# Squared lengths of keys and queries by four 32-column matmuls on partitions of their own

## The chip, the cores and the metric

The kernel runs on one core of one Trainium2 chip. The metric is the device time of one execution in microseconds (us); for the kernel before, it is the median of three runs. The profile that is quoted below comes from a further, profiled execution of the same kernel.

## The reference

Two graph layers work on 1250 nodes with 512 features and 20000 edges. The first one, a convolution over the edges beside an attention with random features, holds the change. Of its attention, this part matters here (`t` stands for the keys or the queries, 8 heads of 64 features, `proj` has 256 rows):

```python
def phi(t, is_query):
    t = t * scale                                   # scale = DH ** (-0.25)
    u = jnp.einsum('bhnd,md->bhnm', t, proj)
    diag = 0.5 * jnp.sum(t * t, axis=-1, keepdims=True)
    if is_query:
        m_ = jnp.max(u, axis=-1, keepdims=True)
    else:
        m_ = jnp.max(u, axis=(-2, -1), keepdims=True)
    return jnp.exp(u - diag - jax.lax.stop_gradient(m_)) / np.sqrt(M) + KEPS
qf = phi(q, True)
kf = phi(k, False) * mask[:, None, :, None]
```

Half the squared length of a head's vector, `diag`, is what the change touches. Only 256 token slots take part in the attention (all nodes have batch number 0, and a slot number is at most 255), so keys, queries and values are computed for 256 tokens. Around this stand layer norms, the sum over edges as a product with an adjacency matrix, the convolution's product, batch norms, and a second layer with two large products.

## The kernel before, in words

A first part sorts out the edges (lines above 1400). Then `sorted_graph` builds the adjacency matrix `adj` in 25 batches of 50 columns: `onehots` makes two one-hot tiles on VectorE (L206), `count` multiplies them on TensorE (ten matmuls, L217), and ScalarE casts the sums into `adj` (L220). The attention's preparation is a generator, `beside`, whose pieces stand between these batches in the text of the program:

- `first_nodes` and `node` turn the normed rows of x into `hT`, features on partitions (`transposed`: four transposes, L226, and a copy on ScalarE, L227; the layer norm's statistics are on VectorE, L96 to L101).
- `features(ed.wk, "k")`: for each block b of 128 features, four matmuls of `wk` with `hT` into a PSUM tile (L245); ScalarE scales it into `tT` (L249) and squares it into `sq` (L251). A matmul with the columns of `half` sums the squares of each of the block's two heads (L248, L253) into rows 2b and 2b+1 of `pd`; the four blocks accumulate in `pd`, 8 partitions by 256 tokens. The matmul of block b-1 stands behind the four matmuls of block b. `pd` is copied to `d8` (L255), turned by two transposes (L259) and copied into `dg` (L260).
- eight `pairs`: scores of the keys (L267, two matmuls with 64 rows each), a copy into `kf` (L333), the maximum `kmx` (L334), a matmul for the values (L337), and statistics of `hT` (`stats`, L325).
- `km1` (L347), its largest value over all tokens (L352, L354, L362) and with it `kb` (L365); `features(wqt, "q")` for the queries; between its pieces the exponentials of `kf` on ScalarE (L376, sixteen of them), and the first two `xn` tiles (`normed`, L289).

Behind that, ten turns of a loop do `query` (L267, L461 to L466), `product` (hw, L422, into a PSUM tile of the pool with two buffers that `count` uses too), `keyvalue` (L449), `degrees` (L431 to L438), `batch`, `turn` (L472) and `attend` (L482).

The order of instructions on an engine is fixed when the kernel is built. `order` (`tc.keep_in_program_order`) pins an instruction behind the one that stands before it in the program on its engine; an instruction without it is placed by the framework's scheduler, which follows the program's order but takes a later instruction when it reckons that an earlier one isn't ready. The eight matmuls with `half` are not pinned. An fp32 matmul appears in the profile as two passes, each a LDWEIGHTS and a MATMUL. The PSUM tiles of this part come from the pool `mm` with four buffers; `sq` and `d8` share one tag of two buffers in SBUF.

Of the kernel before, what the change touches and what calls it, by code (L numbers as in the profile page):

```python
# [11 lines left out]
F32 = mybir.dt.float32  # L12
# [4 lines left out]
AF = mybir.ActivationFunctionType  # L17
# [6 lines left out]
KD = D // 128  # L24
KH = HID // 128
TOK = 256
HEADS, DH, M = 8, 64, 256
# [13 lines left out]
NT = TOK // 128  # L41
# [28 lines left out]
def sorted_graph(ctx: ExitStack, tc: tile.TileContext, ed, x, n1g, n1b, n2g, n2b, wconv, bconv,  # L70
                 wq, wk, wv, wo, proj, eps, w1, b1, g1, be1, w2, b2, g2, be2, out):
    nc = tc.nc
# [5 lines left out]
    ident, epsc = ed.ident, ed.epsc  # L78
    order = tc.keep_in_program_order
# [69 lines left out]
    ap1 = att.enter_context(tc.tile_pool(name="att", bufs=1))  # L149
    ap2 = att.enter_context(tc.tile_pool(name="att2", bufs=2))  # L150
    mm = att.enter_context(tc.tile_pool(name="mm", bufs=4, space=PSUM))
# [33 lines left out]
    wct = weight(wconv, "wconv", ap1, "wconv")  # L185


    half = ap1.tile([128, KD, HEADS], F32, name="half")
    nc.gpsimd.memset(half, 0.0)
    for b in range(KD):  # L190
        for a in range(2):
            nc.gpsimd.memset(half[a * 64:a * 64 + 64, b, 2 * b + a:2 * b + a + 1], 0.5)
    va = ap1.tile([128, NT, HEADS, DH + 1], F32, name="va")
    nc.gpsimd.memset(va, 1.0)

# [40 lines left out]
    def features(wt, name):  # L236

        tT = ap1.tile([128, KD, TOK], F32, name=f"{name}T", tag="tT")
        dg = ap1.tile([128, NT, HEADS], F32, name=f"{name}_dg")

        pd = mm.tile([HEADS, TOK], F32, name="mm")
        for b in range(KD):
            ps = mm.tile([128, TOK], F32, name="mm")
            for k in range(KD):
                nc.tensor.matmul(ps, wt[:, k, b * 128:(b + 1) * 128], hT[:, k, :TOK],  # L245
                                 start=(k == 0), stop=(k == KD - 1))
            if b:
                nc.tensor.matmul(pd, half[:, b - 1, :], sq, start=(b == 1), stop=False)  # L248
            nc.scalar.activation(tT[:, b, :], ps, AF.Copy, scale=DH ** -0.25)  # L249
            sq = ap2.tile([128, TOK], F32, name="sq")  # L250
            nc.scalar.activation(sq, tT[:, b, :], AF.Square)  # L251
            yield
        nc.tensor.matmul(pd, half[:, KD - 1, :], sq, start=False, stop=True)  # L253
        d8 = ap2.tile([HEADS, TOK], F32, name="d8", tag="sq")
        nc.scalar.copy(d8, pd)  # L255
        yield
        ps = mm.tile([128, NT, HEADS], F32, name="mm")
        for t in range(NT):
            nc.tensor.transpose(ps[:, t, :], d8[:, t * 128:(t + 1) * 128], ident[:HEADS, :HEADS])  # L259
        nc.vector.tensor_copy(dg, ps)  # L260
        return tT, dg

    def scores(tT, t, b):
# [28 lines left out]
    def beside():  # L292
# [9 lines left out]
        def node():  # L302
            for j in more:
                nodes([j])
                break

        keys = features(ed.wk, "k")
        try:
            while True:
# [36 lines left out]
        km1 = ap1.tile([128, HEADS], F32, name="km1")  # L346
        nc.vector.tensor_tensor(km1, kmx[:, 0, :], kmx[:, 1, :], ALU.max)  # L347
        queries = features(wqt, "q")
        next(queries)
        stats(len(steps))  # L350
# [160 lines left out]
    for f in range(KD):  # L511
        ps = mm.tile([128, TOK], F32, name="mm")
# [5 lines left out]
    for b in range(KD):  # L518
        ps = mm.tile([128, TOK], F32, name="mm")
# [11 lines left out]
    mm = ctx.enter_context(tc.tile_pool(name="mm2", bufs=8, space=PSUM, reuse_waits="tile"))  # L531
# [33 lines left out]
    for f in range(KD):  # L565
        fs = slice(f * 128, (f + 1) * 128)
        st = tmp.tile([128, 3, 6], F32, name="st")
        for i, (n0, n) in enumerate(BSPLIT if f == KD - 1 else ESPLIT):
            c = slice(n0, n0 + n)
            ps = banks.pop(0)[:, :n] if banks else mm.tile([128, n], F32, name="mm")  # L570
            for part in (hi, lo):
                if part is lo and i == 1 and f > 0:
                    add_rows(f - 1)
                for j, k in enumerate(ROWS):
                    nc.tensor.matmul(ps, part[:k, j, fs], adj[:k, j, c],  # L575
                                     start=(part is hi and j == 0), stop=(part is lo and j == NJ - 1))
            t = p2.tile([128, n], F32, name="t", bufs=3)
            nc.vector.tensor_tensor(t, ps, rdeg[:, c], ALU.mult)

            b = at["bconv"] + f  # L580
# [43 lines left out]
    for g in groups:  # L624
        ps = mm.tile([S, 4, 128], F32, name="mm")
# [282 lines left out]
    a, b = (Dense(ops2, m, KD // 2, o, "b2") for m in range(2))  # L908
# [490 lines left out]
def tile_gnn(ctx: ExitStack, tc: tile.TileContext, x, src, dst, *rest):  # L1399
# [171 lines left out]
    with tc.If(v == 0) as arms:  # L1571
        sorted_graph(tc, ed, x, *rest)
# [33 lines left out]
```

## Time and profile before

| | before |
|---|---|
| median of 3 runs | 376.24 us (375.83 to 377.05) |
| the profiled execution | 377.66 us, of it 375.9 us from the first to the last instruction |
| instructions | 4922 |
| TensorE matmuls (PE) | 357.0 us busy, 95% of the span |
| TensorE weight loads (PEld) | 263.3 us, 70% |
| VectorE (DVE) | 235.6 us, 63% |
| ScalarE (ACT) | 157.4 us, 42% |
| GpSimd (POOL) | 35.4 us, 9% |
| granted TensorE clock | 0.989 of full speed |

A row of a profile names a line of the kernel, an engine, an operation and tiles as out<-in; "128*8 128x256" at a matmul is 128 rows and 8 columns of the array and a moving operand of 128 partitions by 256 elements. Ends of matmuls are modelled, so how long a pass takes is read from the distance between starts, or from the chain of work that ended last, where parts follow each other without overlap. "0.33 <-issue" behind a row is idle time of its engine before it in which nothing that the profile shows was waited for.

### The profile page before, as it was taken

What the parts mean: (1) busy time and instruction counts of PE and PEld (TensorE: products, weight loads), DVE (VectorE), ACT (ScalarE), POOL (GpSimd) and SP (SyncE); (2) the same over time, 40 slices, a digit from 0 to 9 for tenths busy, and PEclk for the clock granted to TensorE, in tenths of its full rate; (3) what the DMA queues carried; (4) which work ended last, traced back from release to release, by engine and by line L of the source; (5) the groups of instructions that cost most, each with busy time, mean ns of one, the idle gap of its engine ahead of it and who ended that gap; (6) DMA issues with size and microseconds to landing.
All of it is one profiled execution on the core that took longest, in us unless ns stands there. A gap on an engine that the chain in (4) does not pass through costs nothing.

```text
span 375.9 us, 4922 instructions
## 1 busy us (share of the span) xinstructions
PE 357.0 (95%) x1840; PEld 263.3 (70%) x1840; DVE 235.6 (63%) x585; ACT 157.4 (42%) x310; POOL 35.4 (9%) x55
## 2 busy tenths in 40 slices
PE   8799989999999999999999999999999999999970
PEld 4665555676566699998768888777777777777750
DVE  6899994649897235687887232182780888212783
ACT  5498549727565360111157312232652542111230
POOL 3000000000000005000000009610062000000000
PEclk9999999999999999999999999999999999999995
DMA  6943020000000471000000000240000000000045
GB/s 200 289 166 128 16 98 0 2 1 2 0 1 2 151 279 67 0 3 0 0 2 0 2 0 1 55 171 0 2 0 1 1 2 0 1 0 2 10 126 144
DMA packets 13285, 18.06 MB, mean 48 GB/s; under 512 B 1341, under 2 KB 6658, under 8 KB 13254
## 3 DMA queue, kind: packets, MB, share of 16 engines
q1 hardware_dynamic: 10622, 16.41, 13.0%
q10 hardware_dynamic: 2632, 1.27, 1.3%
q8 instruction: 16, 0.26, 0.3%
q14 instruction: 15, 0.12, 0.1%
HBM read 15.11 MB, written 2.56 MB: 47 GB/s over the span
## 4 chain that ended last, share of the span: by engine, by line
PE 83%; DVE 11%; ACT 2%; issue 1%; DMA 1%; DVEq 0%
PE mm L764 29%; PE mm L707 12%; PE mm L575 12%; PE hw L422 10%; PE mm L245 3%; PE mm L449 2%; PE mm L521 2%; PE mm L482 2%; PE sc L267 2%; PE acc L217 2%; DVE op L206 1%; DVE xs L894 1%; PE mm L226 1%; PE mm L701 1%; DVE kmx L334 1%; PE mm L472 1%
## 5 line engine op out<-in xcount | busy, mean ns | idle before, releaser
L779 ACT ACTIVATE kept<-mm,vT 128x313 f32<-128x313 f32 x36 | 18.5, 521 | 49.6 <-PE mm L764 48.5
L422 PE MATMUL hw<-wconv,xn 128*128 128x512 f32 (+1 forms) x80 | 37.1, 605 | 0.3 <-ACT adj L220 0.3
L707 PE MATMUL mm<-hi,adj 128*128 128x512 f32 (+2 forms) x100 | 32.2, 400 | 0.5 <-DVE hi L655 0.4
L707 PE MATMUL mm<-lo,adj 128*128 128x512 f32 (+2 forms) x100 | 31.7, 395 | 0.0
L129 ACT ACTIVATE r<-mv,epsc 128x1 f32<-128x1 f32 x16 | 4.7, 292 | 52.1 <-DVE mv L128 52.1
L764 PE MATMUL mm<-hid,w 128*128 128x313 f32 x96 | 25.8, 427 | 0.0
L422 PEld LDWEIGHTS hw<-wconv,xn 128*128 128x128 f32 (+1 forms) x80 | 14.1, 188 | 16.4 <-issue 14.8
L575 PE MATMUL mm<-adj,lo 128*128 128x416 f32 (+3 forms) x120 | 25.1, 355 | 0.0
L575 PE MATMUL mm<-adj,hi 128*128 128x416 f32 (+3 forms) x120 | 25.1, 355 | 0.0
L206 DVE TENSOR_TENSOR op<-iop,prow 128x1280 f16<-128x1280 f16 (+2 forms) x27 | 20.8, 769 | 6.0 <-PE acc L217 5.6
L784 DVE TENSOR_TENSOR hid<-mm,kept 128x313 f32<-128x313 f32 x24 | 10.9, 477 | 20.4 <-ACT kept L779 16.9
L764 PEld LDWEIGHTS mm<-hid,w 128*128 128x128 f32 x96 | 18.2, 190 | 6.9
L575 PEld LDWEIGHTS mm<-adj,hi 128*128 128x128 f32 x120 | 21.9, 189 | 1.1
L575 PEld LDWEIGHTS mm<-adj,lo 128*128 128x128 f32 x120 | 21.8, 189 | 1.0
L707 PEld LDWEIGHTS mm<-hi,adj 128*128 128x128 f32 (+2 forms) x100 | 18.4, 186 | 5.8 <-DVE hi L655 1.4
L698 DVE SCALAR_TENSOR_TENSOR z<-h,e,mm 128x512 f32<-128x512 f32 (+1 forms) x10 | 7.0, 745 | 23.5 <-PE mm L707 15.7
L707 PEld LDWEIGHTS mm<-lo,adj 128*128 128x128 f32 (+2 forms) x100 | 18.5, 186 | 4.6 <-DVE lo L648 0.2
L217 PEld LDWEIGHTS <-op 128*128 128x128 f16 x250 | 13.7, 97 | 9.1 <-issue 4.7
L217 PE MATMUL acc<-ok,op 128*128 128x100 f16 x250 | 16.2, 208 | 3.4 <-DVE ok L206 2.7
L784 DVE TENSOR_TENSOR o<-mm,kept 128x313 f32<-128x313 f32 x12 | 5.7, 482 | 21.5 <-ACT kept L779 20.8
L702 ACT COPY zT<-mm 128x512 f32<-128x512 f32 (+1 forms) x10 | 5.3, 583 | 29.3 <-PE mm L701 29.3
L764 PE MATMUL mm<-tz,w 128*128 128x313 f32 x64 | 17.5, 426 | 0.0
(249 smaller groups left out, 717.0 us busy)
## 6 DMA issues: line engine op xcount, KB each, us to landing
w<-in_L_gnn_W_dram SPq DMA_DIRECT2D x2, 2048.0 KB
xs<-in_x_dram SPq DMA_DIRECT2D x1, 2304.0 KB
wk<-in_L_gnn_Wk_dram SPq DMA_DIRECT2D x1, 1024.0 KB
x<-in_x_dram SPq DMA_DIRECT2D x1, 1024.0 KB
v<-in_L_gnn_Wv_dram SPq DMA_DIRECT2D x1, 1024.0 KB
wconv<-in_L_gnn_W_conv_dram SPq DMA_DIRECT2D x1, 1024.0 KB
wk<-in_L_gnn_Wq_dram SPq DMA_DIRECT2D x1, 1024.0 KB
o<-in_L_gnn_Wo_dram SPq DMA_DIRECT2D x1, 1024.0 KB
```

What stands on the lines that cost most here:

```text
L206: i = nc.vector.tensor_tensor(t[:, qs], iota.unsqueeze(1).to_broadcast(shape), keys[:, bt, qs].unsqueeze(2).to_broadcast(shape), ALU.is_equal)
L217: nc.tensor.matmul(acc[:, :, q * TG:(q + 1) * TG], op[:, q, :, i], ok[:, q, :, i].rearrange("p (j t) -> p j t", t=TG), start=(q == 0 and i ...
L245: nc.tensor.matmul(ps, wt[:, k, b * 128:(b + 1) * 128], hT[:, k, :TOK], start=(k == 0), stop=(k == KD - 1))
L267: nc.tensor.matmul(ps[:, a, :M], tT[a * 64:a * 64 + 64, b, t * 128:(t + 1) * 128], projT[a * 64:a * 64 + 64, :], start=True, stop=True)
L422: nc.tensor.matmul(ps[:n], xn[:, f, :n], wct[:, f, :], start=(f == 0), stop=(f == KD - 1))
L449: nc.tensor.matmul(ps[:, i, :], kf[:, t, hd, mb * 128:(mb + 1) * 128], va[:, t, hd, :], start=(t == 0), stop=(t == NT - 1))
L482: nc.tensor.matmul(pa[:, i, :], qfTs[n][:, i, mb, :], kv[:, mb, hd, :], start=(mb == 0), stop=(mb == 1))
L575: nc.tensor.matmul(ps, part[:k, j, fs], adj[:k, j, c], start=(part is hi and j == 0), stop=(part is lo and j == NJ - 1))
L707: nc.tensor.matmul(ps[:n], adj[:k, j, t * S:t * S + n], part[:k, j, :], start=(part is hi and j == 0), stop=(part is lo and j == NJ - 1))
L764: order(nc.tensor.matmul(banks[i], left[:, k, m * 128:(m + 1) * 128], right[:, k, i * NH:(i + 1) * NH], start=(p in (1, 2, 5) and k == 0), ...
L779: nc.scalar.activation(t[:, c, :], self.A[c], AF.Identity, bias=self.part(i, 0, c)[1], scale=1.0)
L784: order(nc.vector.tensor_tensor(self.part(i, j, c)[0], self.B[c], t[:, c, :], ALU.add))
```

## The change

The four blocks no longer accumulate in one tile of 8 partitions. `half` becomes one tile of 32 columns, of which two are filled, and all blocks use it; the squares of all four blocks stay in one tile `sq`; after the last block four matmuls, each with 32 columns, write partitions 32b to 32b+31 of a `pd` with 128 partitions, pinned behind each other with `order`. The copy `d8`, the transposes and the last copy handle 128 partitions, of which the copy to `dg` takes two columns in each 32. Six of nine memsets on GpSimd go.

```diff
-    half = ap1.tile([128, KD, HEADS], F32, name="half")
+    QUAD = 128 // KD
+    half = ap1.tile([128, QUAD], F32, name="half")
     nc.gpsimd.memset(half, 0.0)
-    for b in range(KD):
-        for a in range(2):
-            nc.gpsimd.memset(half[a * 64:a * 64 + 64, b, 2 * b + a:2 * b + a + 1], 0.5)
+    for a in range(2):
+        nc.gpsimd.memset(half[a * 64:a * 64 + 64, a:a + 1], 0.5)
...
-        pd = mm.tile([HEADS, TOK], F32, name="mm")
+        sq = ap2.tile([128, KD, TOK], F32, name="sq", bufs=1)
         for b in range(KD):
             ps = mm.tile([128, TOK], F32, name="mm")
             for k in range(KD):
                 nc.tensor.matmul(ps, wt[:, k, b * 128:(b + 1) * 128], hT[:, k, :TOK],
                                  start=(k == 0), stop=(k == KD - 1))
-            if b:
-                nc.tensor.matmul(pd, half[:, b - 1, :], sq, start=(b == 1), stop=False)
             nc.scalar.activation(tT[:, b, :], ps, AF.Copy, scale=DH ** -0.25)
-            sq = ap2.tile([128, TOK], F32, name="sq")
-            nc.scalar.activation(sq, tT[:, b, :], AF.Square)
+            nc.scalar.activation(sq[:, b, :], tT[:, b, :], AF.Square)
             yield
-        nc.tensor.matmul(pd, half[:, KD - 1, :], sq, start=False, stop=True)
-        d8 = ap2.tile([HEADS, TOK], F32, name="d8", tag="sq")
+        pd = mm.tile([128, TOK], F32, name="mm")
+        for b in range(KD):
+            order(nc.tensor.matmul(pd[b * QUAD:(b + 1) * QUAD], half, sq[:, b, :], start=True, stop=True,
+                                   skip_group_check=True))
+        d8 = ap2.tile([128, TOK], F32, name="d8", bufs=1)
         nc.scalar.copy(d8, pd)
         yield
-        ps = mm.tile([128, NT, HEADS], F32, name="mm")
+        ps = mm.tile([128, NT, KD, QUAD], F32, name="mm")
         for t in range(NT):
-            nc.tensor.transpose(ps[:, t, :], d8[:, t * 128:(t + 1) * 128], ident[:HEADS, :HEADS])
-        nc.vector.tensor_copy(dg, ps)
+            nc.tensor.transpose(ps[:, t], d8[:, t * 128:(t + 1) * 128], ident)
+        nc.vector.tensor_copy(dg.rearrange("p t (b a) -> p t b a", a=2), ps[:, :, :, :2])
         return tT, dg
```

## The prediction

> **What bounds the kernel now.** I read the page's slices and the engines of its chain first, then a table of the stages around the change, then the timeline of TensorE at each place that the change touches, then who waits for whom.
>
> ```profile
> PE   8799989999999999999999999999999999999970
> ...
> DVE  6899994649897235687887232182780888212783
> ...
> PE 83%; DVE 11%; ACT 2%; issue 1%; DMA 1%; DVEq 0%
> ```
>
> A slice is 9.4 us. TensorE carries 83% of the chain that ended last, and from 53 us on hardly anything else does until the tail. So TensorE time saved early should reach the end, unless another engine sets the pace where it is saved. In slices 2 to 6, where keys and queries are made, VectorE reads 8 or 9 too. Hence the table (columns: start:end, length, then busy PE, PEld, DVE, ACT, POOL):
>
> ```profile
> 16.00:38.00 22.00, 21.38 (x147) 14.22 (x147) 20.97 (x59) 18.70 (x44) 0.77 (x7) 1.00 0.50 169
> 38.00:53.20 15.20, 13.22 (x102) 7.51 (x100) 15.06 (x35) 8.51 (x17) 0.00 (x0) 1.00 0.19 69
> 53.20:63.15 9.95, 9.70 (x60) 5.95 (x56) 4.34 (x12) 7.26 (x17) 0.00 (x0) 1.00 0.01 2
> 63.15:69.20 6.05, 6.05 (x33) 3.35 (x33) 4.87 (x9) 6.05 (x16) 0.00 (x0) 1.00 0.00 0
> 69.20:128.00 58.80, 58.77 (x359) 37.94 (x357) 41.91 (x99) 31.54 (x73) 0.00 (x0) 1.00 0.01 4
> ```
>
> The keys' features lie in the first row, the scores of the keys in the second, the queries' features in the third. In the first, TensorE is idle 0.6 us and VectorE 1.0 of 22: two full engines. In the second VectorE is full and TensorE idle for 2.0 us. In the third TensorE is full, and ScalarE is from 55.5 us on. From 63.15 to 128 TensorE is never idle.
>
> **What TensorE pays for one matmul with `half` today.** The starts show it (the granted clock is full in all these rows):
>
> ```profile
> 21.94 0.38 PE L245 MATMUL mm<-hT,wk 128*128 128x256 f32 x1
> 22.25 0.60 PE L248 MATMUL mm<-sq,half 128*8 128x256 f32 x2
> ...
> 22.25 0.10 PEld L248 LDWEIGHTS mm<-sq,half 128*8 128x8 f32 x2 [0.33 <-issue]
> 22.77 0.31 PEld L226 LDWEIGHTS mm<-ident,hn 128*128 128x128 f32 x3 [0.43 <-ACT kT L249]
> ```
>
> A pass over 256 elements takes 0.216 us (in the chain, eight passes of L245 take 1.73). The last L245 pass starts at 21.94, so the next could at 22.15; L248 starts at 22.25. Its two passes would let L226 start at 22.68; it starts at 22.77, with its weights not loaded ahead, which costs 0.06 more. So 0.43 of work carries 0.10 on the way in and 0.15 on the way out: 0.68 us. Its square had been ready since 18.7, so that is no wait for data. The keys' other three cost the same (0.68 each), the queries' four 0.62, 0.73, 0.64 and 0.63 by the same reading (at 55.43, 58.19, 60.64, 62.10). Eight make 5.3 us.
>
> The two transposes of `d8`, on 8 rows of the array, behave alike:
>
> ```profile
> 63.15 1.13 PE L422 MATMUL hw<-wconv,xn 128*128 128x512 f32 x2 [0.25 <-ACT adj L220]
> 64.20 0.29 PE L259 MATMUL mm<-ident,d 8*128 8x8 f32 x2
> 64.42 1.12 PE L422 MATMUL hw<-wconv,xn 128*128 128x512 f32 x2
> ```
>
> The two L422 passes from 63.15 on could be followed at 64.11; L422 goes on at 64.42, its first pass 0.10 slower: 0.42 us for the queries, and 0.31 for the keys by the same reading. All in all 6.0 us.
>
> **The change part by part.** *Four matmuls at once.* No row shows four groups of columns side by side. The nearest row is L267, two matmuls on two halves of the rows:
>
> ```profile
> 33.13 0.49 PE L267 MATMUL sc<-projT,kT 64*128 64x256 f32 x2
> ...
> 33.13 0.70 PE L267 MATMUL sc<-projT,kT 64*128 64x256 f32 x4
> 33.77 0.70 PE L337 MATMUL mm<-v,hT 128*128 128x512 f32 x1
> ```
>
> The first row is cut at 33.2: two passes have started by then, 7 ns apart; all four are over in time for L337 at 33.77. Two matmuls took the time of one. If columns behave like rows, one visit costs 0.10 in, 2 x 0.216, three times 0.007, about 0.03 for loading 32 columns instead of 8 (8 columns took 87 ns, 128 took 190), and 0.15 out: 0.74 us.
>
> A rule of the Trainium skill speaks against it: "TensorE: Matmul & The Clock Gate", The mechanism, says a weight load runs beside matmuls in flight only when the row group differs, and here all four use all rows. Against its wording stands L245: in one row group, at 0.216 us a pass, no load is exposed. By the rule, eight passes of 0.216 + 0.09 and 0.25 make 2.70 us a visit. The same page (Measured speedup vs the span model) gives 2.38 times for three column groups. Between lie passes that overlap only with the neighbour's (five slots: 1.36) and passes in sequence with hidden loads (2.01). I take 0.74, by the nearest row, and keep 2.70 as the other end. Switching in and out is in all of them; "TensorEngine Tiling (Array Packing)", Key Properties, says that changing the mode drains the engine, which is the 0.10 of the rows above.
>
> *Transposes.* Now 128 rows and columns, like L226, which needs 0.11 each and, outside a switch, nothing in or out: 0.22 instead of 0.42 and 0.31, although sixteen times as many elements move.
>
> *Sum on TensorE.* A features stage goes from 3.0 us to 0.74 + 0.22 = 0.96. Saved: 2.0 for keys, 2.1 for queries, 4.1 together; with 2.70 a visit, 0.2.
>
> *The rest.* The copy `d8` covers 128 partitions (0.36 us; a copy of the same 256 elements on 128 partitions, L249, 0.38): 0.04 on ScalarE in all. The last copy keeps its 16 elements (0.17). Six memsets of 0.092 leave GpSimd at 9.3 to 10.4 us; it is then idle for 8 us, so 0, and uncovered they would be a gain. No DMA moves or is added; SP passes nothing new. `pd` holds a PSUM buffer only at the end of the stage, which frees one of four before: 0 to a gain, apart from the rival below. The pin puts the first `pd` matmul behind the last of the ten L217 before it in the program; in the keys L253 already ran right behind such a group, in the queries that batch's ten were over at 61.6, before L253 at 62.10: 0. All four now wait for the last square; behind the first one on TensorE wait `d8`, the transposes and `q_dg` (65.05), which nobody needs before the query's 65.72. If VectorE or ScalarE did not cover these, the order would cost up to the 0.5 us between the squares and L253.
>
> **What of it reaches the end.** *Keys (2.0).* VectorE is the second full engine, and it waited for TensorE only here:
>
> ```profile
> DVE op L206 <- PE acc L217: 0.4, 1, 0.4
> DVE oh L431 <- PE mm L226: 0.3, 1, 0.3
> ```
>
> That 0.7 can go. Beyond it a gain needs a new order on VectorE: it runs fill-in between 37 and 49 us that belongs later (two L431 and L601, 0.9; L289, 1.7), and has 5.2 us free for it from 56.6 on. Bounds 0.3 and 2.0; I take 0.8. The next late thing is VectorE's `kmx`.
>
> *Queries (2.1).* TensorE's next large work, L422 at 63.15, takes a PSUM buffer that ScalarE frees with the cast at 62.53 (0.25 idle before it, in the fence above). ScalarE runs from 55.53 to there without a hole but 0.12 and 0.18 us before L249, and its work stays: the cast can come 0.3 earlier. The transposes inside L422's stretch give 0.2 more. Later the exponentials end at 67.0, and work that needs them (L267 at 68.56, L449 at 69.19) has some 0.8 of slack. Bounds 0.3 and 2.1; I take 0.6.
>
> Sum: 1.4 us. The profiled execution took 377.66, 1.76 more than its span of 375.9 and 1.42 more than the median; it would become 376.3, its span 374.5, and the median 376.24 - 1.4 = 374.8.
>
> **The rivals.** *B, all of it arrives* (0.12): the scheduler, seeing a free TensorE and PSUM buffer, moves query blocks into the 2.0 us that TensorE idles before 53. For it: it did so with block 0 (L245 at 45.96). Against: it left block 1 at 53.60. Gain 2.4 to 4.1; 372.9.
>
> *C, hidden or not there* (0.18): columns don't overlap (0.2 saved), or VectorE and ScalarE eat the whole. For it: both full. Time 376.2, 0.7 either way.
>
> *D, slower* (0.18): blocks of queries (1.73 us each) moved early stand in front of scores L267 between 48 and 53 us, where `kmx`, then `kb` and all exponentials hang on them. Price: the block less TensorE's holes there (0.45, 0.62, 0.80), some 1.1 a block. It decides from the second block on: 2.3 late on the exponentials, 0.8 of slack there: 1.5 slower, 377.7. Against: TensorE recovers that work after 53.
>
> **How the numbers follow.** My own sum, A, has 0.52, with 373.8 to 375.5 as its range. Under 0.3%, 1.1 us, a measurement of this kernel can't be told from no change. Faster by more: three quarters of A, all of B, a little of C: 0.54. Slower: most of D and a little of C: 0.18. The rest is 0.28. The range leaves out the best of B and the worst of D: 372.6 to 377.4.
>
> **What would show it.** Right: the four `pd` matmuls within some 30 ns at each pass, one visit of 0.7 to 0.8 us per stage, transposes at 0.11 without an idle before them, L347 (53.21) earlier by 0.8 and L422 (63.15) by 1.4, the rows after 69 shifted and otherwise alike. Wrong: visits over 1.3 us; L347 unmoved or late; a longer idle of TensorE before L422; a query block ahead of the last scores.

## The result: slower by 0.35%, and the profile after

| | before | after |
|---|---|---|
| median of 22 runs each | 376.97 us | 378.07 us |
| ratio of the runs | | 1.0035 (95% interval 1.0019 to 1.005) |
| the profiled execution | 377.66 us, span 375.9 | 377.87 us, span 376.1 |
| TensorE matmuls busy | 357.0 us | 356.4 us |
| mean granted TensorE clock | 0.989 | 0.984 |

The kernel after is slower; the prediction was 374.8 us and its range ended at 377.4. The single runs of every kernel here, the one before too, lie in two groups about 2 us apart (in the profiled ones the first L245 starts at 13.7 to 14.0 us in the lower group and at 15.4 to 16.1 us in the upper), so where single runs are compared below, the lower group of each is meant. That group has its median at 376.13 us before (376.1 to 376.2 in each later comparison) and at 377.69 us after.

The page of the kernel after, busy tenths in slices of 9.4 us, and the chain by engine:

```profile
PE   7799978999999999999999999999999999999971
...
DVE  6998985649897325687887232182780888312783
...
PEclk9999989999999999999999999999999999999995
...
PE 81%; DVE 9%; ACT 4%; DMA 1%; issue 1%; SPq 0%; DVEq 0%
```

Slice 6 (47 to 56 us) is new in two rows: TensorE reads 7, where it read 8 before, and the granted clock has an 8 in a row that was all 9 before but for the end. The start of an execution moves by up to 2.5 us from trace to trace, so places are compared from the first L245 on. Of the kernel before:

```profile
15.53 1.97 PE L245 MATMUL mm<-hT,wk 128*128 128x256 f32 x8
...
53.49 0.27 PE L352 MATMUL mm<-ident,km 128*8 128x128 f32 x1
...
53.60 1.89 PE L245 MATMUL mm<-hT,wk 128*128 128x256 f32 x8
```

The kernel after starts its first L245 at 14.00; its other rows stand further down.

| us from the first L245 | before | after | |
|---|---|---|---|
| last L245 of the keys starts | 12.25 | 10.98 | 1.27 earlier |
| L352 (the largest key value's transpose) | 37.96 | 38.97 | 1.01 later |
| first L422 | 47.62 | 49.70 | 2.08 later |
| end of the span | 360.35 | 362.08 | 1.73 later |

So the change did its work in the first 11 us, lost 2.3 us between there and L352, and lost another 1.1 us before L422; 0.35 us came back behind it. Two things happened. TensorE of the kernel after, where the keys' features end (start, length, row):

```profile
26.26 0.63 PE L252 MATMUL mm<-sq,half 128*32 128x256 f32 x6
26.82 0.66 PE L226 MATMUL mm<-ident,hn 128*128 128x128 f32 x4
27.41 0.62 PE L252 MATMUL mm<-sq,half 128*32 128x256 f32 x2
...
28.52 0.70 PE L267 MATMUL sc<-projT,kT 64*128 64x256 f32 x2
29.15 0.44 PE L259 MATMUL mm<-ident,d 128*128 128x128 f32 x2
...
30.77 0.70 PE L267 MATMUL sc<-projT,kT 64*128 64x256 f32 x2
...
33.44 0.70 PE L267 MATMUL sc<-projT,kT 64*128 64x256 f32 x2
34.06 0.66 PE L226 MATMUL mm<-ident,hn 128*128 128x128 f32 x4
34.65 0.70 PE L267 MATMUL sc<-projT,kT 64*128 64x256 f32 x2
```

Three `pd` matmuls run in the time of one, but the fourth comes in a visit of its own (a visit is a run of such matmuls with what it costs to go over to them and back). And the framework's scheduler laid out everything behind the features anew: two pairs of key scores are split. A pair together took 0.63 us (x4); each half by itself takes the same. VectorE's waits of the kernel after, from 14 to 53 us (total, times, longest), to be held against the two rows in the prediction:

```profile
DVE op L206 <- PE acc L217: 1.5, 2, 0.8
DVE kmx L334 <- ACT kf L333: 0.6, 2, 0.3
DVE k_dg L260 <- PE mm L259: 0.2, 1, 0.2
```

VectorE is idle 2.6 us between the first L245 and L352 (before: 1.2). It has 0.4 us less work there (36.4 us busy instead of 36.8; one of 24 one-hot tiles comes later), and 1.4 less 0.4 is the 1.0 us at L352.

The second thing is the clock. The same table as in the prediction, over three stretches of 3.41 us in front of and behind L352 (columns: start:end, length, busy PE, PEld, DVE, ACT, POOL, then the granted clock), of the kernel after:

```profile
46.39:49.80 3.41, 2.55 (x31) 1.57 (x29) 3.27 (x11) 1.61 (x3) 0.00 (x0) 1.00 0.55 211
49.80:53.22 3.42, 1.75 (x20) 1.06 (x17) 3.42 (x9) 1.79 (x4) 0.00 (x0) 1.00 0.00 0
53.22:56.63 3.41, 3.41 (x10) 2.23 (x8) 2.18 (x6) 0.03 (x1) 0.00 (x0) 0.50 0.02 5
```

and of the kernel before:

```profile
47.02:50.44 3.42, 2.97 (x33) 1.98 (x31) 3.42 (x8) 1.64 (x3) 0.00 (x0) 1.00 0.68 261
50.44:53.85 3.41, 1.99 (x21) 1.15 (x18) 3.41 (x9) 1.79 (x4) 0.00 (x0) 1.00 0.00 0
53.85:57.26 3.41, 3.41 (x17) 2.39 (x16) 2.38 (x7) 1.68 (x3) 0.00 (x0) 1.00 0.02 5
```

After a stretch in which TensorE was busy 1.75 us the clock is 0.50 for one stretch; after one with 1.99 us it is not. It hits the second block of the queries, which TensorE's chain cannot spare:

```profile
52.34 0.70 PE L267 MATMUL sc<-projT,qT 64*128 64x256 f32 x4 [1.05 <-DVE kmx L334]
52.97 0.27 PE L352 MATMUL mm<-ident,km 128*8 128x128 f32 x1
53.08 3.48 PE L245 MATMUL mm<-hT,wk 128*128 128x256 f32 x8
...
63.71 1.12 PE L422 MATMUL hw<-wconv,xn 128*128 128x512 f32 x2 [1.00 <-ACT adj L220]
```

The eight passes of L245 behind L352 take 3.48 us here and 1.89 us before (row at 53.60). Of the 22 runs after, 21 have a mean clock of 0.982 to 0.984, one 0.986; in the largest later comparison 70 of 75 runs before stand at 0.986 to 0.990.

### The profile page after: what moved, and what is told of

Same layout as the page of the kernel before. It is cut to its first block, busy times and chain, and to the rows that moved or that the text cites. A ratio compares the mean times of both kernels' runs of the same rounds, so it can differ in the third digit from the quotient of the medians.

```text
span 376.1 us, 4914 instructions
## 1 busy us (share of the span) xinstructions
PE 356.4 (95%) x1840; PEld 263.6 (70%) x1840; DVE 235.9 (63%) x585; ACT 157.1 (42%) x310; POOL 34.9 (9%) x49
## 3 DMA queue, kind: packets, MB, share of 16 engines
q10 hardware_dynamic: 2632, 1.27, 1.3%
## 4 chain that ended last, share of the span: by engine, by line
PE 81%; DVE 9%; ACT 4%; DMA 1%; issue 1%; SPq 0%; DVEq 0%
PE mm L764 29%; PE mm L707 12%; PE mm L575 12%; PE hw L422 10%; PE mm L245 3%; PE sc L267 2%; PE mm L521 2%; PE mm L449 2%; PE mm L482 2%; PE acc L217 2%; DVE xs L894 1%; PE mm L701 1%; PE mm L337 1%; DMA x<-in_x_dram 1%; PE mm L226 1%; PE mm L472 1%
## 5 line engine op out<-in xcount | busy, mean ns | idle before, releaser
L422 PE MATMUL hw<-wconv,xn 128*128 128x512 f32 (+1 forms) x80 | 37.0, 604 | 1.0 <-ACT adj L220 1.0
L422 PEld LDWEIGHTS hw<-wconv,xn 128*128 128x128 f32 (+1 forms) x80 | 14.1, 187 | 17.8 <-issue 14.8
L764 PE MATMUL mm<-hid,sw 128*128 128x313 f32 x64 | 17.5, 426 | 0.0
```

The source lines that it names most:

```text
L422: nc.tensor.matmul(ps[:n], xn[:, f, :n], wct[:, f, :], start=(f == 0), stop=(f == KD - 1))
L764: order(nc.tensor.matmul(banks[i], left[:, k, m * 128:(m + 1) * 128], right[:, k, i * NH:(i + 1) * NH], start=(p in (1, 2, 5) and k == 0), ...
```

## The experiments

Two theories were tried against each other. The *clock theory*: TensorE, with less to do where VectorE sets the pace, falls below some share of busy time, is given half the clock for 3.41 us, and pays for it in the next stage. The *order theory*: the new order (split pairs, late counts) starves VectorE. A third, that columns side by side are dearer than rows, fell with the traces: the `pd` passes start 7 ns apart.

### Counts issued twice, in the kernel after

```diff
-        for q in range(BG):
+        for q in [*range(BG)] * (2 if bt in (11, 12) else 1):
...
```

> The changed kernel, with the ten count matmuls (L217) of batches 11 and 12 issued twice each (the first round is overwritten), so that TensorE has 0.46 us more to do in each of its two largest holes before 53 us (0.86 before the score pair of L267 at 49.34, and 1.05 before the one at 52.34). The order of all instructions on all engines up to the second layer stays that of the changed kernel. Theory 1 (the half clock of 3.41 us that the trace shows from 53.22 on comes from TensorE's holes before it and costs about 1.1 us): the half clock is gone, L352 to L422 shrinks from 10.7 to about 9.7 us, and the time falls by 1.0 to 1.5 us, although TensorE does 0.9 us more. Rival (the half clock is a matter of the run's phase, or is hidden behind ScalarE's queue): time within 0.3 us of the changed kernel or above it.

377.49 us median, ratio 1.0009 (0.9992 to 1.0026). The second set of ten matmuls begins the sum anew, so the result does not change; TensorE has 0.9 us more to do. Its two stretches ahead of L352:

```profile
50.25:53.67 3.42, 1.95 (x28) 1.25 (x24) 3.42 (x7) 2.27 (x5) 0.00 (x0) 1.00 0.01 5
53.67:57.08 3.41, 3.26 (x17) 2.42 (x18) 3.41 (x13) 0.73 (x3) 0.00 (x0) 1.00 0.02 5
```

With 1.95 us busy the clock stays. L352 is where it was after (+38.98), so the order theory's loss is still there, but L422 comes at +48.13 instead of +49.70, and the span ends 1.37 us earlier from the first L245. The lower group's runs split by their clock: ten at 0.988 to 0.990 have a median of 376.59 us, six at 0.982 or 0.983 of 377.8 us. Doing more work made the kernel faster. What is left against before, 0.46 us by the runs and 0.36 by the traces, belongs to the order.

### Fewer counts, in the kernel before

```diff
+        last = 0 if bt in (10, 11, 12) else 1
         for q in range(BG):
-            for i in range(2):
+            for i in range(last + 1):
...
```

> The kernel before, with the counts of the batches 10, 11 and 12 halved: only one of the two matmuls of each group is issued (5 instead of 10 of L217 a batch), so that their counts are half missing. TensorE has about 0.7 us less work (15 matmuls of 0.046 us), all of it between 47 and 53.5 us, where it waits for VectorE; the order on TensorE and on VectorE stays that of the kernel before. Clock theory: TensorE's busy time in the 3.41 us before 54 us falls from about 2.0 us to about 1.5 us, the next such stretch is then granted half the clock, and the kernel gets slower by about 1 us although it does less: ratio 1.002 to 1.004, mean granted clock 0.983 instead of 0.989 in most runs. Order theory (only the sequence of the instructions matters): nothing is late, so the ratio is 0.998 to 1.000 and the clock 0.989.

378.15 us, ratio 1.0024 (1.0003 to 1.0045). Half of the counts of three batches are left out, so `adj` is incomplete. The order of TensorE is that of before and L352 stays at +37.96, to the hundredth; the clock changes:

```profile
48.79:52.20 3.41, 1.77 (x16) 1.03 (x13) 3.41 (x9) 1.76 (x4) 0.00 (x0) 1.00 0.00 0
52.20:55.62 3.42, 3.42 (x10) 1.85 (x8) 2.04 (x4) 0.44 (x2) 0.00 (x0) 0.50 0.02 5
```

L422 is 1.64 us later than before, the end 1.60 us. Ten of the 22 runs had it (most were expected to), at a mean clock of 0.978 to 0.984: in the lower group three at 377.5 to 377.6 us, beside seven at 0.986 to 0.990 with a median of 376.15 us, as before. The price of one stretch at half clock in this place is 1.4 us by the runs and 1.6 by the traces, in a kernel without any of the change. That a half-clock stretch costs the time, and that the work of TensorE ahead of it brings or removes it, is shown both ways round.

### No squared lengths at all

```diff
-            if b:
-                nc.tensor.matmul(pd, half[:, b - 1, :], sq, start=(b == 1), stop=False)
...
-        nc.tensor.matmul(pd, half[:, KD - 1, :], sq, start=False, stop=True)
...
-        nc.scalar.copy(d8, pd)
+        nc.scalar.copy(d8, sq[:HEADS])
```

> The kernel before, leaving out all eight matmuls with half (d8 is a copy of squares instead, so the squared lengths are wrong): 5.3 us less work on TensorE, more than the change saves. If TensorE sets the pace here, as the prediction had it: 2 to 5 us faster. Theory 1: the keys' part of the saving ends in holes before 53 us, a half clock follows, and the time is within 1.5 us of the kernel before. Theory 2 (slow by the changed order): faster by 2 us or more, as no pair of L267 is split in this one.

The squared lengths are then not computed at all; `d8` is a copy of squares. 378.35 us is the median of all 22 runs; the ratio, 1.0 (0.9976 to 1.0025), is that of the 15 up to 379.4 us. All eight matmuls with `half` are gone, and nothing is won, as the clock theory had it; the order theory had expected 2 us or more. L422 comes at +46.38 in the trace, 1.2 us earlier than before, in spite of this:

```profile
45.79:49.20 3.41, 1.72 (x24) 1.26 (x24) 3.41 (x6) 1.95 (x5) 0.00 (x0) 1.00 0.00 0
49.20:52.61 3.41, 3.40 (x12) 2.22 (x10) 2.58 (x9) 0.71 (x2) 0.00 (x0) 0.50 0.02 5
52.61:56.03 3.42, 3.42 (x10) 2.39 (x9) 1.33 (x5) 1.62 (x2) 0.00 (x0) 0.50 0.00 0
```

Two stretches at half clock. The runs show the staircase: the only one at 0.989 took 373.9 us, those at 0.986 and 0.982 took 374.8 and 374.9, those at 0.980 begin at 376.5, those at 0.973 at 377.9. By that one run, all the sums could bring with the clock left alone is some 2.2 us (376.1 to 373.9).

### The columns at the old places

Against the kernel before; `half`, `pd`, the copies and the transposes are those of the kernel after.

```diff
...
-                nc.tensor.matmul(pd, half[:, b - 1, :], sq, start=(b == 1), stop=False)
+                nc.tensor.matmul(pd[(b - 1) * QUAD:b * QUAD], half, sq, start=True, stop=True, skip_group_check=True)
...
```

> The kernel before, with one part of the change alone: each block's squares are summed by a matmul of 32 columns onto partitions of their own, at the place where the kernel before does it (behind the next block's four matmuls), so no visit to the array is saved and no matmuls lie side by side; copy and transposes with 128 partitions. Theory 1 (time goes where TensorE is freed): TensorE's visits are as dear as before, the time is within 0.5 us of the kernel before and there is no half clock. Theory 2 (the new order that the scheduler finds, with score pairs of L267 split in two, makes it slow): the order around the keys' scores changes here too (one pair is split), so up to 1 us slower without any half clock.

380.69 us (six runs), ratio 1.0093 (1.0059 to 1.0127), more than either theory had allowed for, though TensorE does about as much as before. Features end as before (+12.29), L352 comes at +39.84, 1.9 us late, with VectorE idle 2.8 us on the way, and the clock is halved from 53.77 on: both theories' losses without the gain. One pair of scores is split in this order too.

### Only the place

The four squares are kept and summed behind the last block, still in 8 rows, accumulating, without columns.

```diff
-            if b:
-                nc.tensor.matmul(pd, half[:, b - 1, :], sq, start=(b == 1), stop=False)
...
+        for b in range(KD):
+            order(nc.tensor.matmul(pd, half[:, b, :], sq[:, b, :], start=(b == 0), stop=(b == KD - 1)))
...
```

> The kernel before, with only the place changed: the four squares of a stage are kept, and the four half matmuls are issued after the last block as in the kernel after, but they still add up in 8 rows (no columns of the array, transposes of 8 rows). No score pair is split in its order. If columns are what costs, this one is faster than before by the early features: L352 at +37 us, ratio 0.995 to 0.998. If the new place is what costs (features done 1.3 us early, a larger hole of TensorE before 54 us, half clock), it is slower like the kernel after: ratio 1.001 to 1.004 and clock 0.983 in most runs. Order theory: about 0.999 to 1.001, since no pair is split but nothing else is won either.

377.0 us, ratio 0.9983 (0.9964 to 1.0001). Its order has no split pair, L352 comes at +37.80, the clock stays full in the profiled run, and the span ends 0.7 us earlier than before from the first L245. The nine lower runs (0.986 or more) have a median of 375.37 us, 0.8 below before. So the new place is not what costs; it wins, without any pin. Its features end as early as those of the kernel after (+10.98), and yet no pair is split: the early end alone did not bring the split order. Which of the other differences (durations, the wider transposes) tipped the scheduler stays open.

### The pairs kept together, in the kernel after

```diff
-            nc.tensor.matmul(ps[:, a, :M], tT[a * 64:a * 64 + 64, b, t * 128:(t + 1) * 128],
-                             projT[a * 64:a * 64 + 64, :], start=True, stop=True)
+            i = nc.tensor.matmul(ps[:, a, :M], tT[a * 64:a * 64 + 64, b, t * 128:(t + 1) * 128],
+                                 projT[a * 64:a * 64 + 64, :], start=True, stop=True)
+            if not qT: order(i)
```

> The kernel after, with the two score matmuls of a pair (L267, keys) kept in program order beside each other, so that none of the eight pairs is split. Order theory: the two visits to the array that the split cost (2 times 0.63 us) go, VectorE is idle about 1.2 us between 20 and 56 us instead of 2.6 us, and L352 comes at +37.8 us from the first L245 instead of +38.97 us; the time falls by about 1 us, ratio 1.000 to 1.002, and by another 1 us if the half clock goes as well. Clock theory alone: the pairs don't matter, L352 stays at +39.0 us and the ratio is 1.003 to 1.004.

375.01 us, ratio 0.9966 (0.9949 to 0.9984): one added pin turns the loss into a gain. All the key scores now stand in program order behind the `pd` matmuls. The starts of VectorE's maxima over the scores (`kmx`, one for each pair) show what changed. Of the kernel after (second pair on):

```profile
32.12 0.69 DVE L334 TENSOR_REDUCE kmx<-sc 128x2 f32<-128x512 f32 x1 [0.26 <-ACT kf L333]
...
36.00 0.69 DVE L334 TENSOR_REDUCE kmx<-sc 128x2 f32<-128x512 f32 x1 [0.31 <-ACT kf L333]
...
39.23 0.68 DVE L334 TENSOR_REDUCE kmx<-sc 128x2 f32<-128x512 f32 x1
...
42.54 0.68 DVE L334 TENSOR_REDUCE kmx<-sc 128x2 f32<-128x512 f32 x1
```

and with the pin (line numbers are one higher there; first pair on):

```profile
30.25 0.67 DVE L335 TENSOR_REDUCE kmx<-sc 128x2 f32<-128x512 f32 x1
...
33.12 0.69 DVE L335 TENSOR_REDUCE kmx<-sc 128x2 f32<-128x512 f32 x1
...
35.86 0.68 DVE L335 TENSOR_REDUCE kmx<-sc 128x2 f32<-128x512 f32 x1
...
38.67 0.68 DVE L335 TENSOR_REDUCE kmx<-sc 128x2 f32<-128x512 f32 x1
```

A pair every 2.7 to 2.9 us, against 3.2 to 3.9 from the second to the sixth pair after. VectorE waits once in the whole stretch, 0.6 us for L259, and L352 is at +37.46, L422 at +46.61, the end 1.25 us earlier than before from the first L245. The half clock is gone as well: all 22 runs are at 0.986 or 0.987, the trace shows full clock from 5 us up to the tail, and TensorE's lowest stretch in the profile ahead of L352 has 2.34 us of 3.41.

### The same pin on the kernel before

The three lines of the edit above, in the kernel before; nothing else.

> Control: the kernel before, with the same pin as in the run with the pairs kept (score matmuls of the keys in program order). No pair was split in it, so the pin moves only the first pair, from the first block of features to behind the last. Order theory with the change's own gain: nothing to win here, ratio 0.999 to 1.001, L352 at +37.6 to +38.2 us from the first L245. Rival, the gain of 0.34% came from the pin and not from the columns: ratio 0.996 to 0.998.

377.97 us, ratio 1.0022 (1.0001 to 1.0043). The pin itself wins nothing: the ten runs of the lower group without a halved clock (0.989 or 0.990) have a median of 376.66 us, 0.5 above before. Its first pair now stands behind all features, which may be the reason. Against it the pinned kernel after stands at 374.78 us: 1.9 us for the change under one and the same pin. (The profiled run lost 1.5 us to a half clock from 15.8 to 19.2 us, in the keys' features.)

### The place alone under the pin

The edit of the run with only the place, and the pin.

> The place alone under the same pin: the four half matmuls at the end of the stage without columns (8 rows, accumulating), and the pairs kept. With the two runs that have the pin on the kernel before (376.4 to 376.9 us where the clock was not halved) and on the kernel after (374.5 to 375.0 us in the same group) it splits the 1.9 us between place and columns. Working: the four matmuls in a row cost 4 times 0.43 and 0.25 us, 1.98 us a stage, the kernel after pays 1.4 us in two visits; so if the columns' saving reaches the end in both stages, this one stands 0.6 to 1.2 us above the kernel after with the pairs kept (375.3 to 376.0 us in that group, ratio 0.998 to 1.000). If place alone does it: 374.6 to 375.0 us, ratio 0.996 to 0.997.

377.03 us, ratio 0.9997 (0.9975 to 1.0019); the five lower runs at 0.986 to 0.990 have a median of 375.49 us, within what was expected if the columns count. So of the 1.9 us, 1.2 come from the place (376.66 to 375.49) and 0.7 from the columns (375.49 to 374.78). The traces agree on the columns: from the first L245 the span ends at 359.60 here and at 359.10 in the pinned kernel after.

### The columns at the old places under the pin

The edit of that earlier run, and the pin.

> The columns at the old places of the half matmuls (one behind each block), with the pin on the pairs. The same without the pin was 0.93% slower, with VectorE idle for 3.1 us between 20 and 56 us and L352 at +39.84 us. Order theory: with no pair split VectorE's idle time falls to about 1.2 us, L352 comes at +37.8 us, ratio 0.998 to 1.002. Rival, columns one at a time cost something of their own: L352 stays beyond +39 us and the ratio above 1.005.

379.01 us, ratio 1.0052 (1.0032 to 1.0072): better than 1.0093, but the order theory had promised 0.998 to 1.002. L352 is at +38.98. The maxima keep the good pace here (seven steps in 19.4 us, as in the pinned kernel after), but the first one starts at +18.11, where the pinned kernel after has +16.59; and the profiled run's clock is halved from 52.73 on. The four lower runs without it (0.988 or 0.989) take 377.2 to 377.6 us, some 0.7 above the pinned kernel before. Of the 1.5 us by which L352 is later than in the pinned kernel after, 1.3 are there at the end of the features (last L245 at +12.29, not +10.98): columns used one block at a time save no visit. What makes it slower than the pinned kernel before stays open.

### All pairs pinned but the first

```diff
-            nc.tensor.matmul(ps[:, a, :M], tT[a * 64:a * 64 + 64, b, t * 128:(t + 1) * 128],
-                             projT[a * 64:a * 64 + 64, :], start=True, stop=True)
+            i = nc.tensor.matmul(ps[:, a, :M], tT[a * 64:a * 64 + 64, b, t * 128:(t + 1) * 128],
+                             projT[a * 64:a * 64 + 64, :], start=True, stop=True); (t or b) and order(i)
```

> The kernel after, with the pin on all pairs but the first. No pair is split here either, but in the order that results three of the four values matmuls of the first block stand ahead of the second pair, and the last pair of the keys comes one batch of counts later than in the run with the pairs kept. If the extra visits of split pairs are what cost: as the run with the pairs kept, L352 at +37.5 us, ratio 0.996 to 0.998. If what counts is how early VectorE and ScalarE get their scores: L352 at +38.5 to +39.5 us and 1.000 to 1.004.

383.22 us (six runs), ratio 1.0159 (1.0124 to 1.0194), worse than either expectation. No pair is split, and it is the slowest of all: the score pairs come behind values and counts, VectorE makes three more one-hot tiles ahead of L352 (27, not 24), which is at +40.19, and the profiled run has four stretches at half clock, two of them in the first layer's loop:

```profile
66.69:70.10 3.41, 2.08 (x23) 1.52 (x21) 2.00 (x3) 3.41 (x9) 0.00 (x0) 1.00 0.00 0
70.10:73.51 3.41, 2.80 (x5) 1.60 (x6) 2.41 (x6) 1.80 (x5) 0.00 (x0) 0.50 0.00 0
```

L352 is 2.2 us later than before, but the first L422 only 0.7 us (+48.29); most of the loss comes behind it, where the half clock is. VectorE is idle no longer than before on the way to L352 (1.2 us), so it is not starved here: it does other work first. So "split pairs" is too narrow a name for the order's part. The traces fit this: what counts is when VectorE gets its scores and how they stand between its one-hot tiles, and the split is one way to spoil that. No run changes this alone.

### One visit, and one visit with counts twice

The `pd` matmul of the last block is issued first, so all four wait for the same square; in the second kernel the counts of batch 12 are issued twice besides.

```diff
-        for b in range(KD):
+        for b in (KD - 1, *range(KD - 1)):
             order(nc.tensor.matmul(pd[b * QUAD:(b + 1) * QUAD], half, sq[:, b, :], start=True, stop=True,
```

> As the run with the pairs kept, and the four half matmuls start with the last block, so that all four of a stage wait for the same square and run together: one visit to the array per stage instead of two. Each stage saves 0.55 us of TensorE; that of the queries lies in front of L422. Order theory: 0.3 to 0.6 us less than the run with the pairs kept, ratio 0.998 to 1.001. Clock theory: TensorE still has its hole before 54 us, clock 0.983 in most runs, and 1 us of it is lost: ratio 1.001 to 1.003.

376.28 us, ratio 0.9965 (0.9946 to 0.9984). The eight lower runs have a median of 374.42 us, 0.36 below the pinned kernel with two visits; four runs at 0.977 or 0.978, the profiled one among them, lost it again to the clock (377.3 to 377.8 us).

> As the run with the pairs kept and one visit, with the counts of batch 12 issued twice (0.46 us more of TensorE in front of the queries' scores, where it waits for VectorE; the order on the other engines is the same). Batch 12 then counts double in this kernel's adjacency. Clock theory: the four runs of 22 that had a half-clock stretch (377.3 to 377.8 us) go; all others as before, lowest time 374.1 to 374.4 us, ratio 0.995 to 0.997. Without a role of the clock: 0.2 to 0.5 us slower than that run, ratio 0.997 to 0.999.

376.25 us, ratio 0.9959 (0.9943 to 0.9976). (Here too the second set begins the sum anew, unlike what I had written.) No run falls under 0.984, none is above 376.62 us, and the seven lower ones have a median of 374.49 us. Its `pd` matmuls in the keys and queries, and its stretches before L352 (its line numbers are one higher behind L267):

```profile
28.94 0.64 PE L252 MATMUL mm<-sq,half 128*32 128x256 f32 x8 [0.42 <-ACT sq L248]
...
60.42 0.64 PE L252 MATMUL mm<-sq,half 128*32 128x256 f32 x8 [0.62 <-ACT sq L248]
62.08 1.13 PE L423 MATMUL hw<-wconv,xn 128*128 128x512 f32 x2 [1.02 <-ACT adj L220]
```

```profile
47.22:50.63 3.41, 2.58 (x30) 1.61 (x26) 3.41 (x8) 1.97 (x4) 0.00 (x0) 1.00 0.46 176
50.63:54.04 3.41, 2.83 (x30) 2.28 (x31) 3.41 (x9) 1.54 (x4) 0.00 (x0) 1.00 0.02 5
```

Four matmuls, eight passes, in 0.64 us, where a single fp32 matmul takes 0.60 (L248 before). This kernel and the two with the pin on the kernel after but no extra counts are faster than before and after; their intervals overlap, so no best one is named.

## Why the prediction was wrong, step by step

*What a visit costs.* Held. In the chain of before a visit to `half` takes 0.53 us and lengthens the transposes behind it from 0.44 to 0.59, which is the 0.68. After, it is 0.56 and again 0.15: 0.71, where 0.74 was written.

*Columns behave like rows.* Held. The row of after, cut at 26.3 us:

```profile
26.26 0.42 PE L252 MATMUL mm<-sq,half 128*32 128x256 f32 x3
```

Three first passes have started by then, 7 ns apart. The 2.70 us that followed from the rule on weight loads in the Trainium skill ("TensorE: Matmul & The Clock Gate", The mechanism) did not come: all four took 0.64 us when they ran together. The measurement decides.

*One visit per stage.* Wrong, a small miss: the fourth square is late, so it is three and one, 1.4 us a stage. Pulled together (the runs above) it is worth 0.2 to 0.4 us at the end (lower groups 374.42 and 374.49 against 374.78; in the traces 358.89 against 359.10).

*Keys: 0.8 of 2.0, bounds 0.3 and 2.0.* This is the first step that failed. The features did end 1.27 us earlier, but L352 came 1.01 us later. The prediction saw that VectorE was full, and that only a new order on it would give more; it did not ask what else a new order could do. The scheduler re-plans all that is not pinned behind the change, and a bound of 0.3 from below excluded a loss without a reason. With the pairs pinned L352 comes 0.5 us earlier: the term was right in sign and 0.3 too large when the order is kept.

*Queries: 0.6 of 2.1.* Right in size: from L352 to L422 it is 9.66 us before, 9.15 us in the kernel after with its counts issued twice, and 9.15 us with the pairs pinned: 0.5. But the kernel after itself takes 10.73 us, and that is the second step that failed: "the granted clock is full in all these rows" was carried over to the kernel after, and a change of the clock was put at nothing. In the runs the clock follows how busy TensorE is; the kernel before stood near the edge (1.99 us of 3.41), and the kernel after has 1.75 us there. Price: 1.1 us by the runs, 1.4 by the traces.

*The sum.* The forecast of 1.4 us is close to what the kernel with the pin gives, 1.25 us in the trace (0.5 at L352, 0.5 from there to L422, 0.2 behind it). That the total fits so well is in part luck: the keys bring 0.3 less than was written, the queries some 0.1 more, and against the kernel before with the same pin the change is worth 1.9 us. The kernel as built adds, by traces, 1.6 us of order (1.25 won against 0.36 lost without the half clock) and 1.4 us of clock: +1.7.

*Costs at nothing.* GpSimd (34.9 us busy instead of 35.4), `d8` (0.36 us) and the pin of the `pd` matmuls cost nothing that shows. The two transposes of the queries' `d8` take 0.22 us from their first start (64.67) to L422's next (64.89), as was written.

*The rivals.* B and C did not come: no further query block moved forward, and the change is not hidden once it is ordered well. D named the right place, the scores between 48 and 53 us, and the right sign, with another mechanism (no query block stands ahead of the scores); that its 377.7 us is close to the 378.07 measured is luck. Two of the signs named for "wrong" came, L347 late and a longer idle of TensorE before L422 (1.00 us for 0.25).

## What to carry to other kernels

Where a scheduler lays out the order, an edit that shortens one stage re-plans the next ones: compare the order of the two programs on every engine before the time is added up, and pin what must stay together. Look at the new order again then: two pins that differ by one pair gave ratios of 0.9966 and 1.0159. Work taken from TensorE in a stretch where another engine sets the pace is not free of effect: add up its busy time per 3.41 us there; in these traces, at 2 us or less the next such stretch was often at half clock, and a few more matmuls in idle time were cheaper than none. When two such effects sit on one gain, test each with a kernel in which the other stays fixed.

## What the runs showed of the hardware that was not expected

The clock falls without any long hole. In the kernel after, the largest hole of TensorE in the stretch ahead of the half clock was 1.05 us; the Trainium skill ("TensorE: Matmul & The Clock Gate", HAM oscillation — how this bites in real kernels) asks for no idle gap beyond about 3.4 us. I laid the 3.41 us grid of each trace's clock changes over its TensorE rows, for the first 80 us of all 14 traces, and took the stretches at full clock. At up to 1.94 us busy of 3.41 the next stretch had half the clock every time (eight stretches: 1.33, 1.57, 1.71, 1.75, 1.77, 1.83, 1.90, 1.94). At 1.95 it went once each way; three at 1.99 or 2.00 stayed full, one at 2.08 fell; from 2.14 on all stayed full, one with a hole of 1.28 us. So in these traces the sum sorts the stretches, the longest hole does not; the edge lies somewhere between 57 and 63% of the recorded busy time, and is no sharp one. Without the transposes the sum sorts them worse (stretches down to 0.88 us stayed full). In two kernels a second stretch at half clock followed the first; in one of them TensorE had been busy for 3.40 us of it, and why it followed there stays open. The grid's place against the program differs from trace to trace, which may be why the same kernel has runs with and without the drop. One stretch costs 1.1 to 1.6 us where TensorE is on the path.

It can also strike early: one profile each of two kernels had it in the keys' features, from 14.1 and from 15.8 us, behind 1.83 and 1.95 us of busy time.
